# Four graph layers on one core: layer 2 of the last two batch pairs as passes of their own, quarter sums made earlier, a planner with other costs

## The chip, the cores and the metric

The kernel runs on one core of one Trainium2 chip. The metric is the device time of one execution in microseconds. Besides the timed runs there is one execution taken by the hardware profiler; views of it are quoted with times from the start of its span. Engines: PE (TensorE), DVE (VectorE), ACT (ScalarE), POOL and SP (which here only issue DMAs).

## The reference

Eight batches of 2048 nodes with 64 channels pass through four residual layers that share one 2048 x 2048 matrix `adj`. All is float32. Cut to what matters:

```python
# layer 0: Chebyshev graph convolution, node-adaptive weights (16 terms per node)
x_g = [x, A @ x, 2 A (A x) - x];  out = sum_d emb[n,d] * (x_g @ weight[d]) + bias
x = layernorm(x + out)
# layer 1: graph attention
e = leaky_relu(s1[:, None] + s2[None, :]); e[adj <= 0.5] = -9e15
x = layernorm(x + elu(softmax(e) @ x))
# layer 2: mean over neighbours
x = layernorm(x + ((adj + I) @ (x @ W.T + b)) / deg)
# layer 3: three steps, node 0 overwritten first
v = x;  v[:, 0] = iv
for _ in range(3):
    v = relu(concat([v, adj @ v]) @ W1.T + b1) @ W2.T + b2
x = layernorm(x + v)
```

## The kernel before

**Tiles.** Batches are taken in four pairs (`NPAIR`), so that two batches of 64 channels fill 128 columns. A slot such as `SX[p]` holds pair p's 2048 nodes as 16 tiles of 128 x 128. A product with the matrix is a *sweep*: the transposed matrix is streamed from HBM in 32 tiles of 128 x 2 x 512 (512 KB each, `fetch`, issued by SP into `a_ring`), chunk by chunk of 512 output nodes (`NCH` = 4) and eight tiles a chunk. Each tile serves two matmuls of 512 columns, each of which the profile shows as two instructions. The result of a chunk stands in one PSUM buffer of `acc_ring` (two) until an evict step copies it out.

**Order of the sweeps** (`sweeps`): first product of layer 0 for pairs 0 and 1 together (`masks=True`: DVE also makes the attention mask and adj + I from each tile); then the second product of pair p = 0 to 3, with the first product of pair p + 1 beside it where there is one left; then, for pairs 0 and 1, one sweep of layer 2 and three of layer 3. The last two pairs (`JOINT`) go together: `joint_layer2` (L1205) takes four matrix tiles at a time, one from each quarter of the matrix, and runs both pairs over each of them; `joint_layer3` (L1277, L1292) does the three steps of layer 3 with seven products of quarters instead of eight. It needs four sums and differences of the quarters (s1 to s4). `sums` (L1165, L1167) makes them on DVE during the joint layer 2 pass and POOL stores them in DRAM. Where a tile holds adj + I instead of adj, `pure` (L1148) fetches it once more.

**Between the sweeps.** `second_pass` (L593) multiplies each node tile by 16 weight blocks; `add_terms` scales the 16 results by the node's embedding and adds them. With a free buffer of `e_ring` (four of 128 x 2048), ACT writes 16 scaled terms (L616) and DVE adds them in a tree (L630, L632); without one, DVE adds each straight to `SX` (L618). For pair 0, ACT makes eight terms and DVE the other eight. `y2_evict` holds a chunk in one of two `yt_ring` buffers until the second pass is through with it. `layer1` and `scores` (L724, the row maxima, with masks loaded into `mr_ring`), `weights` (L802, L810, L815, L818, and the product L828) and `finish` (L863 to L902) are the attention layer. `layer2_tail` (L974, L983), `start_chunk` (norm, transposes L1008, then `u_chunk` L1021), `h_evict` (L946) and `last_chunk` (L1041) follow the sweeps of layers 2 and 3.

**Order of the instructions.** Nothing is ordered by the compiler. All steps are generators that `yield` an engine and what they wait for; `Plan` keeps a model time for each engine and each event, always starts the step that can begin earliest, and among equals the one of the lowest rank, and so fixes the order on every engine's queue. `plan.run(engine, cost, *after)` books a cost. For PE it adds `SLACK` to the time at which a step counts as ready. `sweeps` has rank 1000, so sweeps fill what PE has left. On the chip each engine works through its queue in that order and waits at semaphores.

Of the kernel before, what the change touches and what calls it, by code (L numbers as in the profile page):

```python
# [9 lines left out]
F32 = mybir.dt.float32  # L10
# [7 lines left out]
P = 128  # L18
# [19 lines left out]
class Plan:  # L38
# [6 lines left out]
    SLACK = 2.5  # L45

    def __init__(self):
        self.free = dict.fromkeys(["PE", "DVE", "ACT", "DMA", "SP"], 0.0)
        self.at = {}
        self.threads = []  # L50
        self.count = itertools.count()
# [8 lines left out]
    def run(self, eng, cost, *after):  # L60
        t = max([self.free[eng], *(self.when(a) for a in after)]) + cost
        assert t < NEVER
        self.free[eng] = t
        return t + self.LAG

# [70 lines left out]
def resnorm_d4_kernel(  # L136
# [44 lines left out]
    mr_ring = Ring(wp, "mr", 2)  # L181
# [36 lines left out]
    A_BUFS = 7  # L218
# [7 lines left out]
    def fetch(n):  # L226
        c, q, plus = order_of_a[n]
        t, k = a_ring.take([P, 2, CW], "a")
        freed = a_ring.t
        if isinstance(c, str):  # L230
            src = sum_tiles[c][q]
        else:
            src = a_plus_i[q] if plus and c == q // 2 else tile_of_adj(c, q)
        nc.sync.dma_start(t, src)
        a_tiles[n] = (t, k)
        at["a", n] = plan.run("SP", 1.4, freed) + 3.5
# [23 lines left out]
    blocks = ("w2bd", "w31v", "w31e", "w32bd", "w32c")  # L260
    w2bd, w31v, w31e, w32bd, w32c = (const.tile([P, P], F32, name=n) for n in blocks)
# [107 lines left out]
    def weights_of_l23():  # L369
# [20 lines left out]
        pp_ring.give(k, done)  # L390
        yield "PE", [pp_ring, done]
# [19 lines left out]
    def rows_of_adj():  # L411


        for t in range(NT):
# [4 lines left out]
            done = plan.run("SP", 2.8, bc_ring.t, 115.0 + 9.0 * t) + 9.0  # L419
            plan.start(1, row_tile(t, an, k, done))  # L420

    def row_tile(t, an, k, done):
# [9 lines left out]
        done = plan.run("DVE", 1.13 + 0.16, done)  # L432
        bc_ring.give(k, done)
        nc.gpsimd.dma_start(by_row[t], mk)
        done = plan.run("DMA", 0.6, done) + 4.0
        mr_ring.give(km, done)
        at["by_row", t] = done + 2.0
        if all(("by_row", i) in at for i in range(NT)):
            at["rows"] = done

    def mask_of_tile(n, t, k):
# [7 lines left out]
        if c == q // 2:  # L449
# [6 lines left out]
            got = plan.run("DMA", 0.6, got) + 4.0  # L456
        a_ring.give(k, max(done, got))
        nc.gpsimd.dma_start(by_col[q][:, :, cols(c)], mk)
        done = plan.run("DMA", 0.8, done) + 4.0
        mk_ring.give(km, done)  # L460
        at["by_col", q, c] = done + 2.0

    def layer_norm(v, n, after, centered=False):
# [4 lines left out]
        if not centered:  # L468
# [7 lines left out]
            done = plan.run("DVE", dve(n, 2) + 0.1, after)  # L476
# [9 lines left out]
        done = plan.run("DVE", dve(n) + 0.1, done)  # L486
# [5 lines left out]
        done = plan.run("ACT", 0.3, done)  # L492
        yield "DVE", [done]

        nc.vector.tensor_tensor(vs, vs, r, ALU.mult)
        nc.vector.scalar_tensor_tensor(vs, vs, -0.5, r, ALU.mult, ALU.mult)
        nc.vector.scalar_tensor_tensor(r, vs, 1.5, r, ALU.add, ALU.mult)
        nc.vector.tensor_tensor(v3, v3, r.unsqueeze(2).to_broadcast([P, nb, C]), ALU.mult)
        return plan.run("DVE", dve(n) + 0.4, done)
# [7 lines left out]
    def y1_chunk(p, c, pa, ka, done):  # L507
# [6 lines left out]
        stored = plan.run("DMA", 0.6, done) + 3.0  # L514
        at["y1T", p, c] = stored + 2.0
# [22 lines left out]

    def stacks():

        for n in range(NPAIR * NCH):
            p, c = n // NCH, n % NCH
# [5 lines left out]
            got = plan.run("DMA", 0.6, xg_ring.t, ("y1T", p, c)) + 4.0  # L548
# [15 lines left out]
    def second_pass():  # L564

        for n in range(NPAIR * NCH):
# [4 lines left out]
            for j in range(TPC):  # L571
                t = c * TPC + j
                cs = slice(j * P, (j + 1) * P)
                for h in range(2):
# [5 lines left out]
                    if h == 0 or ring.ready() > plan.free["PE"]:  # L580
                        yield "PE", [("xg", n + 1), got, ring]
                    if h == 0:


                        terms = None
                        if e_ring.ready() < NEVER:
                            terms = e_ring.take([P, D0, P], "terms")
# [17 lines left out]
    def add_terms(p, c, t, h, yp, ring, k, terms, t_pe, left):  # L605

        shared = p == 0 and terms is not None
        eng = "ACT" if terms and not (shared and h) else "DVE"
        yield eng, [t_pe]
        v = SX[p][:, t, :]  # L610
        for d in range(8):
# [5 lines left out]
            else:  # L617
                nc.vector.scalar_tensor_tensor(  # L618
                    batches(v), term, weight, batches(v), ALU.mult, ALU.add
                )  # L620
        done = plan.run(eng, 8 * (0.25 if eng == "ACT" else 0.265), t_pe)
# [4 lines left out]
        if terms:  # L626
            yield "DVE", [done, ("terms", p, t)]
            for half in (4, 2) if shared else (8, 4, 2):
                a, b = (terms[0][:, i * half : (i + 1) * half, :] for i in range(2))
                nc.vector.tensor_tensor(a, a, b, ALU.add)  # L630
            for d in range(2):
                nc.vector.tensor_tensor(v, v, terms[0][:, d, :], ALU.add)  # L632
            done = plan.run("DVE", 1.4 if shared else 2.5, done, ("terms", p, t))
            e_ring.give(terms[1], done)
# [18 lines left out]
    def layer1(p):  # L653
# [7 lines left out]
        for c in range(NCH):  # L661
# [30 lines left out]
        plan.start(10 + p, scores(p, sv, xc, s_rows, done))  # L692

    def scores(p, sv, xc, s_rows, done):
        s2b = []
        for e in range(2):
            yield "DMA", [bc_ring, done, "rows"]
# [4 lines left out]
            ready = plan.run("DMA", 0.8, done, bc_ring.t) + 7.5  # L702
# [6 lines left out]
        def load(t):  # L709
# [4 lines left out]
            at["mask", p, t] = plan.run("DMA", 0.6, mr_ring.t, ("by_row", t)) + 5.0  # L714

        plan.start(1, load(0))
        for h in range(2):
            mx = tiny([P, 2, 8], "mx", 4)
            for t in range(8 * h, 8 * h + 8):
                if t + 1 < NT:  # L720
                    plan.start(1, load(t + 1))
# [20 lines left out]
    def greatest(p, h, mx, sv, xc, s_rows, done):  # L742
# [5 lines left out]
        done = plan.run("DVE", 0.16, done)  # L748
# [7 lines left out]
        for name, rows in (  # L756
# [7 lines left out]
            ready = plan.run("DMA", 0.8, done, bc_ring.t) + 8.0  # L764
# [7 lines left out]
    def to_rows(v, rows, done):  # L772
# [12 lines left out]
        done = plan.run("DMA", 0.5, done) + 2.5  # L785
# [5 lines left out]
    def weights(p, h, jt, s1b, mb, sv, po, ready):  # L791
# [6 lines left out]
        got = plan.run("DMA", 0.6, mk_ring.t) + 4.5  # L798
# [14 lines left out]
        done = plan.run("ACT", act(HALF, 2), done)  # L813
# [6 lines left out]
        mine = held.setdefault((p, h), [])  # L820
        mine.append((jt, e, ke, done))
        if jt % 2 == 0:
            return
        yield "PE", [mine[0][3], done, *([("weighed", p, h, jt - 2)] if jt > 1 else [])]
# [14 lines left out]
        mine.clear()  # L839
# [6 lines left out]
    def finish(p, h, po, kpo, xc):  # L846
# [11 lines left out]
        for f in range(2):  # L858
# [24 lines left out]
            done = plan.run("DVE", dve(CW) + 0.12, t_pe)  # L883
# [21 lines left out]
            done = plan.run("DVE", dve(CW, 2) + 0.2, done)  # L905
# [3 lines left out]
        if h == 0:  # L909
            yield "DMA", [("weighted", p, 1)]  # L910
            nc.gpsimd.dma_start(SX[p][:, 0:8, :], stage)
            done = plan.run("DMA", 1.5, *norms) + 3.0
# [22 lines left out]
    def z_evict(p, c, pa, give, done):  # L935
# [4 lines left out]
        give(done)  # L940
# [29 lines left out]
    def layer2_tail(p, c, z, kz, done):  # L970
# [19 lines left out]
        done = plan.run("DVE", dve(P, TPC) + dve(CW), done)  # L990
# [46 lines left out]
    def last_chunk(p, c, done):  # L1037
# [15 lines left out]
        done = plan.run("DVE", dve(CW, 2), done)  # L1053
# [74 lines left out]
    def order_of_joint():  # L1128
        for k in range(2):
            for r in range(RQ):  # L1130
                order_of_a.extend((c, q, True) for c, q in quarters(k, r))
# [10 lines left out]
    def pure(k, r):  # L1142

        yield "SP", [("group", k, r), *([xg_ring] if len(xg_ring.freed) > 1 else [NEVER])]
        got = []
        for c, q in (quarters(k, r)[i] for i in (0, 3)):
            t, kt = xg_ring.take([P, 2, CW], "pure")
            nc.sync.dma_start(t, tile_of_adj(c, q))  # L1148
            got.append((t, kt, plan.run("SP", 1.4, xg_ring.t) + 4.0))
        return got  # L1150

    def sums(k, r, taken):

        tiles4 = [(t, kt, got) for t, kt, got, _ in taken]
        own = {}
        if r // 2 == k:
            own = dict(zip((0, 3), (yield from pure(k, r))))
        a11, a12, a21, a22 = ((own.get(i) or tiles4[i])[0] for i in range(4))
        ready = [(own.get(i) or tiles4[i])[2] for i in range(4)]

        def out_of(m, a, b, op, *after):
            yield "DVE", [bc_ring, *after]
            t, kt = bc_ring.take([P, 2, HALF], m)
            t = t.rearrange("p a b -> p (a b)")[:, 0 : 2 * CW].rearrange("p (t n) -> p t n", n=CW)
            nc.vector.tensor_tensor(t, a, b, op)  # L1165
            done = plan.run("DVE", dve(2 * CW), *after)
            nc.gpsimd.dma_start(sum_tiles[m][k, r], t)  # L1167
            bc_ring.give(kt, plan.run("DMA", 0.6, done) + 5.0)
            return t, done

        s3, d3 = yield from out_of("s3", a11, a21, ALU.subtract, ready[0], ready[2])
        s1, d1 = yield from out_of("s1", a21, a22, ALU.add, ready[2], ready[3])
        s2, d2 = yield from out_of("s2", s1, a11, ALU.subtract, d1)
        s4, d4 = yield from out_of("s4", a12, s2, ALU.subtract, d2)
        for (_, kt, _, free), d in zip(taken, (d2, d4, d1, d1)):
            a_ring.give(kt, max(free, d))
        for _, kt, _ in own.values():
            xg_ring.give(kt, d2)
        refill()

    def joint_layer2():
        p, o = JOINT
        at["group", 0, 0] = 0.0
        for k in range(2):
            pas = {}
            for r in range(RQ):
                taken = []
                for i, (c, q) in enumerate(quarters(k, r)):
                    n = next(used)
                    if r == 0 and i in (0, 2):  # L1190
                        if i == 0:
                            yield "PE", [po_ring, ("x2", p), ("x2", o)]
                            t2, kp = po_ring.take([P, 2, CW], "po")
                            pas[c] = [(t2[:, e, :], kp) for e in range(2)]
                        else:
                            pas[c] = []
                            for e in range(2):
                                yield "PE", [acc_ring]
                                pas[c].append(acc_ring.take([P, CW], "acc"))
                    for e, pair in enumerate(JOINT):  # L1200
                        yield "PE", [("a", n)]
                        t, kt = a_tiles[n]
# [268 lines left out]
```

## Time and profile before

| | us |
|---|---|
| median of 3 runs | 2172.77 (2169.68 to 2172.82) |
| the profiled execution | 2177.32 |
| its span | 2175.5 |
| PE / DVE / ACT busy in it | 2090.3 / 1532.3 / 933.5 |
| granted TensorE clock in it, mean | 0.984 |

In the profile the sweeps lie so: the first products 6 to 130 us, second products (with the next pair's first) 130 to 944, layer 2 and 3 of pair 0 944 to 1325, of pair 1 to 1685, joint layer 2 1688 to 1814, joint layer 3 to 2163. Attention of the four pairs runs on DVE and ACT from 351 to about 1700. In a line of a group, "x" is the count, then come busy time, the mean of one in ns, and the idle time of the engine before. A matmul's shown length overlaps its successor's; their pace is read from start to start.

### The profile page before, as it was taken

The page shows a single profiled execution, that of the slowest core. Times are in us where ns is not written, and L with a number is a line of the kernel's source. Part 1 is how long each engine was busy: PE and PEld are TensorE (multiplying, and loading weights), DVE is VectorE, ACT ScalarE, POOL GpSimd, SP SyncE. Part 2 cuts the span into 40 slices and gives each one's busy share as a digit, 9 for nine tenths or more (in the row PEclk, how much of TensorE's full clock was granted, in tenths as well). Part 3 has the DMA queues.
Part 4 walks back from the last instruction along what each step waited for, and adds up shares of the span by engine and source line. Part 5 has one row for each costly group of instructions (what it writes and reads, how often), then busy time and mean ns, then how long its engine had stood idle before and what let it go on. Part 6 is the DMA issues. An engine that isn't in the chain of part 4 may idle for free. (4 is left out here: it accounts for less than half of the span.)

```text
span 2175.5 us, 19004 instructions
## 1 busy us (share of the span) xinstructions
PE 2090.3 (96%) x6325; PEld 923.0 (42%) x6325; DVE 1532.3 (70%) x2057; ACT 933.5 (43%) x1605; POOL 213.3 (10%) x374
## 2 busy tenths in 40 slices
PE   8998999999999999999998999989999998999997
PEld 3443444333433333344443444434444454444443
DVE  2226756999799999979998978989797555020214
ACT  0014433476576457767624746417566012000001
POOL 2211001100110110001001011011100110000000
PEclk9999999999999999999999999989999999999999
DMA  9798845633542475446688788778687687878785
GB/s 313 270 328 305 287 133 184 216 107 96 162 150 88 150 234 153 146 126 198 223 289 299 247 286 294 233 249 303 220 293 226 238 301 243 281 251 282 252 291 169
DMA packets 208739, 495.85 MB, mean 228 GB/s; under 512 B 20274, under 2 KB 28594, under 8 KB 204530
## 3 DMA queue, kind: packets, MB, share of 16 engines
q1 hardware_dynamic: 165058, 347.62, 48.3%
q0 software_dynamic: 39360, 144.92, 19.4%
q10 hardware_dynamic: 4224, 2.10, 0.4%
q8 instruction: 50, 0.82, 0.1%
q14 instruction: 47, 0.39, 0.1%
HBM read 446.14 MB, written 46.33 MB: 226 GB/s over the span
## 5 line engine op out<-in xcount | busy, mean ns | idle before, releaser
L1086 PE MATMUL acc<-a,SX 128*128 128x512 f32 x1024 | 470.1, 603 | 9.0 <-DMA SX<-in_x 6.4
L1086 PE MATMUL acc<-a,SA 128*128 128x512 f32 x768 | 352.9, 602 | 8.0 <-ACT SA L348 4.7
L810 ACT ACTIVATE e<-e,sv 128x1024 f32<-128x1024 f32 x256 | 280.4, 1153 | 123.6 <-DVE e L802 117.3
L724 DVE CUSTOM_DVE_ANT_0 junk<-s2b,mr 128x2048 bf16<-128x2048 f32 x128 | 292.7, 2287 | 32.6 <-DMA mr<-by_row 31.3
L818 ACT ACTIVATE e<-e 128x2048 f32<-128x2048 f32 x128 | 245.3, 1925 | 120.5 <-DVE e L815 120.2
L802 DVE TENSOR_TENSOR e<-s1b,mk 128x2048 f32<-128x2048 f32 x128 | 289.6, 2284 | 9.8 <-DMA mk<-by_col 9.8
L815 DVE TENSOR_TENSOR e<-e,mb 128x2048 f32<-128x2048 f32 x128 | 290.2, 2284 | 7.6 <-ACT e L810 7.5
L1086 PEld LDWEIGHTS acc<-a,SX 128*128 128x128 f32 x1024 | 191.7, 193 | 242.7 <-issue 229.1
L593 PE MATMUL yp<-SH,xgT 128*128 128x512 f32 x512 | 250.7, 615 | 1.8 <-DVE SX L618 1.0
L616 ACT ACTIVATE terms<-yp,emb_sb 128x128 f32<-128x128 f32 x768 | 207.9, 396 | 70.9 <-PE yp L593 70.6
L828 PE MATMUL po<-e,SX 128*64 128x512 f32 x1024 | 234.0, 599 | 3.0 <-ACT e L818 3.0
L1086 PEld LDWEIGHTS acc<-a,SA 128*128 128x128 f32 x768 | 142.6, 192 | 182.0 <-issue 168.3
L1292 PE MATMUL acc<-a,t 128*128 128x512 f32 x384 | 169.1, 592 | 0.0
L593 PEld LDWEIGHTS yp<-SH,xgT 128*128 128x128 f32 x512 | 92.4, 193 | 147.6 <-issue 139.0
L593 PE MATMUL yp<-SH,y2T 64*128 64x512 f32 x512 | 134.9, 634 | 17.3 <-ACT terms L616 9.8
L630 DVE TENSOR_TENSOR terms<-terms 128x512 f32<-128x512 f32 (+1 forms) x152 | 111.2, 731 | 35.6 <-ACT terms L616 32.2
L828 PEld LDWEIGHTS po<-e,SX 128*64 128x64 f32 x1024 | 68.0, 137 | 155.6 <-issue 137.8
L797 POOL DMA_DIRECT2D mk<-by_col x128 | 69.3, 542 | 589.4 <-DVE e L802 475.9
L618 DVE SCALAR_TENSOR_TENSOR SX<-yp,emb_sb,SX 128x128 f32<-128x128 f32 x256 | 89.7, 350 | 48.9 <-PE yp L593 40.4
L1086 PE MATMUL acc<-a,SB 128*128 128x512 f32 x256 | 120.1, 601 | 0.0
L1292 PEld LDWEIGHTS acc<-a,t 128*128 128x128 f32 x384 | 72.0, 190 | 86.1 <-issue 86.1
L480 ACT ACTIVATE ln_sq<-SX 128x512 f32<-128x512 f32 x48 | 30.4, 633 | 146.4 <-DVE SX L473 81.1
(226 smaller groups left out, 1704.2 us busy)
## 6 DMA issues: line engine op xcount, KB each, us to landing
a<-in_adj_t SPq DMA_DIRECT2D x496, 512.0 KB, 5.3
a<-s SPq DMA_DIRECT2D x96, 512.0 KB, 4.5
mr<-by_row POOLq DMA_DIRECT2D x64, 512.0 KB, 5.9
mk<-by_col POOLq DMA_DIRECT2D x128, 256.0 KB, 5.6
an<-in_adj SPq DMA_DIRECT2D x16, 1024.0 KB, 9.3
s<-s POOLq DMA_DIRECT2D x32, 512.0 KB, 6.9
a<-a_plus_i SPq DMA_DIRECT2D x24, 512.0 KB, 5.7
by_col<-mk POOLq DMA_DIRECT2D x32, 256.0 KB, 6.1
```

The lines of the kernel that those rows point to most:

```text
L593: nc.tensor.matmul(yp[:, e, :], lhsT=y2T[rows, cs] if k2 else xg[:, e, cs], rhs=(wk2 if k2 else w01)[rows, hs], start=(k2 == h), stop=(k2 ...
L616: nc.scalar.activation(batches(terms[0][:, dd, :]), term, AF.Copy, scale=weight)
L618: nc.vector.scalar_tensor_tensor(batches(v), term, weight, batches(v), ALU.mult, ALU.add)
L630: nc.vector.tensor_tensor(a, a, b, ALU.add)
L724: nc.vector.tensor_tensor_reduce(out=junk, in0=s2b[e][0], in1=masks[t][0], scale=1.0, scalar=LOWEST, op0=ALU.add, op1=ALU.max, accum_out=m ...
L802: nc.vector.tensor_tensor(e, s1b[0], mk.unsqueeze(1).to_broadcast([P, 2, HALF]), ALU.add)
L810: nc.scalar.activation(e[:, i, :], e[:, i, :], AF.Prelu, bias=sv[:, 2 + i, jt : jt + 1], alpha=ALPHA)
L815: nc.vector.tensor_tensor(e, e, mb[0], ALU.add)
L818: nc.scalar.activation(e, e, AF.Exp)
L828: nc.tensor.matmul(po[i * C : (i + 1) * C, f, :], lhsT=SX[p][:, t, i * C : (i + 1) * C], rhs=e[:, i, f * CW : (f + 1) * CW], start=(t == 0 ...
L1086: nc.tensor.matmul(pa, lhsT=source[:, m, :], rhs=t[:, i, :], start=(m == 0 and not seed), stop=(m == NT - 1),)
L1292: nc.tensor.matmul(pa, lhsT=B[:, 2 * r + b, :], rhs=at_[:, b, :], start=(r == 0 and b == 0 and not go_on), stop=(r == RQ - 1 and b == 1), ...
```

## The change

Layer 2 of pairs 2 and 3 becomes two ordinary sweeps. The sums of quarters are made in place, in the tiles themselves, during the second product of pair 3 (`SUMS`), which for that takes the tiles by quarters and finishes chunks 0 and 2, then 1 and 3. `a_ring` goes from seven buffers to six, `mr_ring` from two to three. The second pass always has a terms buffer and waits for it; the tree of adds becomes one reduction over the 16 (or 8) terms. In the norm, a DVE multiplication becomes a squaring on ACT. `Plan` gets a model of shared DMA bandwidth, other costs, a smaller `SLACK` and other ranks. Of the cost changes only some are shown.

```diff
     LAG = 0.3
-    SLACK = 2.5
+    RATE = 340.0
+    SLACK = 1.0
...
+    def dma(self, queue, kb, *after):
+        t = self.run(queue, 0.4 if queue == "SP" else 0.7, *after) - self.LAG
+        self.moved = max(t + 3.5, self.moved) + kb / self.RATE
+        return self.moved + 0.2
...
-    mr_ring = Ring(wp, "mr", 2)
+    mr_ring = Ring(wp, "mr", 3)
...
-    A_BUFS = 7
+    A_BUFS = 6
...
-        at["a", n] = plan.run("SP", 1.4, freed) + 3.5
+        at["a", n] = plan.dma("SP", 512, freed)
...
         nc.scalar.activation(r, r, AF.Exp, scale=-0.5)
-        done = plan.run("ACT", 0.3, done)
+        rr = tiny([P, nb], "ln_rr", 2)
+        nc.scalar.activation(rr, r, AF.Square)
+        done = plan.run("ACT", 0.55, done)
         yield "DVE", [done]
-        nc.vector.tensor_tensor(vs, vs, r, ALU.mult)
-        nc.vector.scalar_tensor_tensor(vs, vs, -0.5, r, ALU.mult, ALU.mult)
+        nc.vector.scalar_tensor_tensor(vs, vs, -0.5, rr, ALU.mult, ALU.mult)
...
                     if h == 0 or ring.ready() > plan.free["PE"]:
-                        yield "PE", [("xg", n + 1), got, ring]
+                        yield "PE", [("xg", n + 1), got, ring, *([e_ring] if h == 0 else [])]
                     if h == 0:
-                        terms = None
-                        if e_ring.ready() < NEVER:
-                            terms = e_ring.take([P, D0, P], "terms")
+                        terms = e_ring.take([P, D0, P], "terms")
...
-        shared = p == 0 and terms is not None
-        eng = "ACT" if terms and not (shared and h) else "DVE"
+        shared = p == 0
+        eng = "DVE" if shared and h else "ACT"
...
-                nc.vector.scalar_tensor_tensor(
-                    batches(v), term, weight, batches(v), ALU.mult, ALU.add
-                )
+                to = batches(terms[0][:, d, :])
+                nc.vector.scalar_tensor_tensor(to, term, weight, to, ALU.mult, ALU.add)
...
-            for half in (4, 2) if shared else (8, 4, 2):
-                a, b = (terms[0][:, i * half : (i + 1) * half, :] for i in range(2))
-                nc.vector.tensor_tensor(a, a, b, ALU.add)
-            for d in range(2):
-                nc.vector.tensor_tensor(v, v, terms[0][:, d, :], ALU.add)
+        n = 8 if shared else D0
+        added = tiny([P, P], "added", 1)
+        nc.vector.tensor_reduce(
+            added, terms[0][:, 0:n, :].rearrange("p d n -> p n d"), AX.X, ALU.add
+        )
+        nc.vector.tensor_tensor(v, v, added, ALU.add)
...
-        plan.start(10 + p, scores(p, sv, xc, s_rows, done))
+        plan.start(1.2 if p == 0 else 9.5 + p, scores(p, sv, xc, s_rows, done))
...
-            yield "DMA", [bc_ring, done, "rows"]
+            yield "DMA", [bc_ring, done]
...
         plan.start(1, load(0))
+        plan.start(1, load(1))
...
+    def sweep_with_sums(source, evict, need):
+        for k in range(2):
+            pas = {}
+            for r in range(RQ):
+                group = []
+                for i, (c, q) in enumerate(quarters(k, r)):
+                    n = next(used)
+                    if r == 0 and i in (0, 2):
+                        yield "PE", [acc_ring]
+                        pas[c] = acc_ring.take([P, CW], "acc")
+                    yield "PE", [("a", n), *need(q // 2)]
+                    t, kt = a_tiles.pop(n)
+                    for b in range(2):
+                        nc.tensor.matmul(
+                            pas[c][0],
+                            lhsT=source[:, 2 * q + b, :],
+                            rhs=t[:, b, :],
+                            start=(r == 0 and i in (0, 2) and b == 0),
+                            stop=(r == RQ - 1 and i in (1, 3) and b == 1),
+                        )
+                    done = plan.run("PE", mm(CW, 2), ("a", n), *need(q // 2))
+                    if r == RQ - 1 and i in (1, 3):
+                        plan.start(1, evict(c, *pas[c], done))
+                    group.append((t, kt, done))
+                    if i == 3:
+                        plan.start(0, sums(k, r, group))
+                    refill()
+
+    def sums(k, r, group):
+        (a11, _, d11), (a12, _, d12), (a21, _, d21), (a22, _, d22) = group
+        for i, m, out, a, b, op, after in (
+            (3, "s1", a22, a21, a22, ALU.add, (d21, d22)),
+            (2, "s3", a21, a11, a21, ALU.subtract, (d11, d21)),
+            (0, "s2", a11, a22, a11, ALU.subtract, (d11,)),
+            (1, "s4", a12, a12, a11, ALU.subtract, (d12,)),
+        ):
+            yield "DVE", after
+            nc.vector.tensor_tensor(out, a, b, op)
+            done = plan.run("DVE", dve(2 * CW) + 0.03, *after)
+            nc.gpsimd.dma_start(sum_tiles[m][k, r], out)
+            a_ring.give(group[i][1], plan.dma("DMA", 512, done))
+        refill()
...
             products = [second_product(p)]
+            if p == SUMS:
+                yield from sweep_with_sums(*second_product(p)[0:3])
+                continue
...
+        yield from sweep(layer2_product(NPAIR - 2))
         yield "PE", [("x2", NPAIR - 1)]
         h_o, _ = e_ring.take([P, 2, HALF], "h_o")
-        yield from joint_layer2()
+        yield from sweep(layer2_product(NPAIR - 1))
         yield from joint_layer3()
```

## The prediction

> **What bounds the kernel now.** I read the page first (busy shares and the forty slices), then busy time by stage, then the waits of PE, then the timeline of PE around the stage that is rebuilt, and last the groups by shape, for prices.
>
> The page: PE is busy nearly everywhere, DVE only from about slice 7 to 31.
>
> ```profile
> PE 2090.3 (96%) x6325; PEld 923.0 (42%) x6325; DVE 1532.3 (70%) x2057; ACT 933.5 (43%) x1605; POOL 213.3 (10%) x374
> ...
> PE   8998999999999999999998999989999998999997
> DVE  2226756999799999979998978989797555020214
> ```
>
> Busy time by stage (window, its length, then PE, PEld, DVE, ACT, POOL busy, granted clock, DMA share, GB/s):
>
> ```profile
> 150.00:350.00 200.00, 193.49 (x563) 82.74 (x561) 120.70 (x311) 85.41 (x227) 14.54 (x25) 0.98 0.71 249
> 350.00:1050.00 700.00, 679.95 (x2084) 274.82 (x2084) 650.49 (x816) 443.80 (x912) 71.24 (x129) 0.99 0.49 156
> 1050.00:1684.00 634.00, 607.34 (x1963) 269.06 (x1960) 560.72 (x550) 337.74 (x339) 67.82 (x122) 0.98 0.77 263
> 1684.00:1850.00 166.00, 154.22 (x483) 80.23 (x482) 90.12 (x172) 26.32 (x60) 17.87 (x33) 0.96 0.75 260
> 1850.00:2176.00 326.00, 314.12 (x874) 150.72 (x872) 75.60 (x138) 27.83 (x52) 6.04 (x8) 0.99 0.77 254
> ```
>
> PE idles 6.5, 20.1, 26.7, 11.8 and 11.9 us in these stages, 85 us in all with the start. The change neither adds nor removes a product: joint layer 2 is 128 matmuls, two passes are 2 x 64. So PE's work stays, and only its idle time and what follows it can move. The waits of PE (total, times, longest):
>
> ```profile
> PE yp L593 <- ACT terms L616: 10.6, 6, 5.7
> PE ps_vT L1008 <- DVE SX L498: 8.3, 2, 6.8
> ...
> PE ps_u L1021 <- ACT SH L946: 5.2, 1, 5.2
> ...
> PE po L1205 <- DVE SX L498: 3.4, 1, 3.4
> ```
>
> The second and last of these lie at the two ends of the joint pass. PE's timeline there (start, length, group, idle before):
>
> ```profile
> 1688.12 5.31 PE L1205 MATMUL po<-a,SX 128*128 128x512 f32 x12
> 1696.81 2.65 PE L1205 MATMUL po<-a,SX 128*128 128x512 f32 x4 [3.37 <-DVE SX L498]
> 1699.25 8.11 PE L1205 MATMUL acc<-a,SX 128*128 128x512 f32 x16
> 1707.19 7.03 PE L1205 MATMUL po<-a,SX 128*128 128x512 f32 x16
> ...
> 1818.34 1.05 PE L974 MATMUL ps_emb<-w2bd,z 128*128 128x128 f32 x8
> 1826.20 2.32 PE L1008 MATMUL ps_vT<-ident,SX 128*128 128x128 f32 x8 [6.81 <-DVE SX L498]
> 1829.96 2.08 PE L1021 MATMUL ps_u<-w31e,SH 128*128 128x128 f32 x8 [1.44 <-ACT SH L348]
> ```
>
> An undisturbed run of 16 takes 6.87 us start to start (1707.19 to the next group), 0.429 per instruction; the 16 after the first wait take 7.94. A wait like this one is followed by a slow stretch and costs more than itself.
>
> **1. The ends of the joint pass.** At the front, 1688.12 to 1707.19 is 19.07 us for 32 instructions worth 13.73: 5.3 us lost to pair 3's last norm (x2 of the last pair). Afterwards PE has pair 2's layer 2 to run instead, 128 instructions or 55 us, so x2 may come up to some 50 us later unseen. At the back, from 1819.2 (the four ps_emb groups done) to 1834.4 (steady again) are 15.2 us for 12 transposes at 0.11 and 16 ps_u at 0.112, 3.1 us: 12.1 lost, because both pairs' last chunks must pass copy, norm, transpose and u before the first product can go on. Afterwards the first two products of layer 3 read pair 2's u alone, made a pass earlier; they hold 64 instructions, 27.5 us, over the 15 us chain of pair 3's last chunk. I take both away: **-17.4 us**. If the cover fails, the same 12 come back.
>
> **2. The sums on DVE.** 32 subtractions and additions of 128x1024 move from the joint pass, where DVE idles, to the sweep of pair 3 (771 to 944 in the timeline), where it is 95% busy: 32 x 1.22 = 39 us. They go at rank 0, ahead of terms and weights. DVE is relieved in the second pass at the same time. Prices:
>
> ```profile
> L618 DVE SCALAR_TENSOR_TENSOR SX<-yp,emb_sb,SX 128x128 f32<-128x128 f32 x256 | 89.7, 350 | 48.9 <-PE yp L593 40.4
> L630 DVE TENSOR_TENSOR terms<-terms 128x1024 f32<-128x1024 f32 x40 | 48.8, 1219 | 32.3 <-ACT terms L616 32.2
> L632 DVE TENSOR_TENSOR SX<-SX,terms 128x128 f32<-128x128 f32 x112 | 32.7, 292 | 3.9
> L1165 DVE TENSOR_TENSOR s<-a,s 128x1024 f32<-128x1024 f32 x8 | 9.8, 1224 | 1.3 <-DMA s<-s 1.2
> ```
>
> A tile's tree of adds is 1.219 + 0.689 + 0.425 (the other two shapes of L630) + 2 x 0.292 = 2.92 us. One reduction of 2048 elements has no row; the nearest are the 2048-element addition (2.28) and the reduction of 512 (0.68), so 2.28, and 2.57 with its addition. 40 tiles x 0.35 = 14 us less. Eight tiles that had no buffer go from 16 x 0.35 = 5.6 to 2.57: 24 less, against 128 more ACT instructions at 0.27 = 35 us on an engine busy 43%. Pair 0's sixteen: 3 less. Each of 64 norms loses a DVE instruction of 0.16 and gains one of 0.21 on ACT. Up to 1050 us DVE is therefore even: 39 - 14 - 24 - 3 - 4 = -6.
>
> The reduction reads its 16 terms 512 bytes apart. The trace has one DVE instruction with such a step, the copy of each batch's last column (32 elements, 256 bytes apart):
>
> ```profile
> L686 DVE COPY xc<-SX x4: 184/188/192, 330.9 to 1314.7; 128x32 f32<-128x32 f32 x4
> ```
>
> From additions of 512 (0.690) and 2048 (2.284) an element costs 1.04 ns and an instruction 158; 32 elements would be 191, and double price per element 224. It took 188, so I charge no step; the dear end is sixteen separate 128x128 additions, 16 x 0.292 = 4.67 us a tile, 2.1 more. The Trainium skill speaks against this ("Advanced Engine Details and Errata", SBUF Cachelines): an access that lands on another 16-byte line each time pays a penalty. It gives no figure; were the penalty a doubling, an estimate from that rule, the sum on DVE would be +100 instead of -6. The row, though short, shows no penalty.
>
> **3. Who waits for PE's sake.** A second-pass tile must now find an e buffer before it starts, where before it took one that was not yet free or went to DVE directly. That answers yp <- ACT terms (10.6), ps_xg <- ACT terms (2.2), ps_sv <- ACT terms (0.7), yp and ps_xg <- DVE SX (1.9 and 2.4): 17.8 us with the slow stretches on top, 25 at most; but the 5.7 at 196 us is in pair 0's pass, which stays. Bounds 0 and -25, I take **-9**.
>
> **4. Buffers.** In the quarter sweep four tiles are held together until four sums (4.9 us) and a store (s<-s lands after 6.9) are over, 11.8 us in which two of six buffers serve, 3.4 us of matmuls. Eight groups x 8.4 = 67 us if PE had nothing else. In the stretch 771 to 944 this sweep was 55 us of PE's 173; the rest is second pass and weights. By that share 21 us would show; most can be fetched while PE does the rest: bounds 0 and 67, I take **+5**. Six buffers instead of seven in the first sweep, where DMA is at 0.94 to 0.98 for 75 us and the matrix waits are 5.8 us in the whole run: 0 to +6, **+1**. The matrix is fetched 32 times more, 16.8 MB, and the 8 pure fetches on SP go; a dense pass needs 0.524 MB per 1.72 us = 305 GB/s, and 293 was moved without a wait in 1875 to 1900 us.
>
> **5. Scores of pair 0 ahead of the terms (rank 10 to 1.2), a third mr buffer.** Their 32 x 2.29 = 73 us can now run as one block from 351 us. Meanwhile pair 1's reductions wait, its four e buffers fill, and PE has 4 tiles x 5.4 + some 34 us of sweep before two yT buffers are used up: 56 of 73. Bounds 0 and +20, **+4**.
>
> **6. The order as a whole.** PE's margin goes from 2.5 to 1.0 us, most costs are raised by 0.1 to 0.35 and DMAs share a modelled 340 GB/s. Of the 47 us idle between 350 and 1684, part comes from work that the plan put too early. The smaller margin pulls the other way. No row prices it: bounds -35 and +25, I take **-10**.
>
> Sum: -17.4 - 9 + 5 + 1 + 4 - 10 = -26.4. The profiled execution took 2177.3 (span 2175.5), so 2150.9; it is 4.5 above the median of the runs, so I say **2147 us**.
>
> **Rivals.** (a) *Buffers decide, slower.* Place: the quarter sweep. Price 67 us in full. It decides once over 26 of them (40%) show; at 70%, 2147 + 42 = 2189. For: DVE is 95% busy there, and a late sum holds four of six buffers. Against: two thirds of PE's work there needs none. 20%. (b) *The score block gives the gain back*: 20 us instead of 4, and the plan's 10 not gained: 2147 + 16 + 10 = 2173, no change. 6%. (c) *The reduction costs as much as separate additions*: 48 x 2.1 + 16 x (8 x 0.292 - 1.51) = 114 us more of DVE before 1050; it idles 50 there from 350 on, so the second pass ends some 65 later; if PE's later fillers hide a third, 2147 + 43 = 2190. 6%. (d) The forecast, with the ends of the joint pass gone: 68%, 2115 to 2165 alone.
>
> Against a resolution of 0.2% (4.3 us) this gives faster 0.68, same 0.06, slower 0.26. The range 2110 to 2196 leaves out the far end of (a) and (c) and a plan that gains all of its 35.
>
> **What would show it.** Right: no wait of ps_vT on DVE before the first layer-3 product, no wait of pair 2's layer 2 on x2; L616 x896, one reduction per tile near 2.28 us; PE idle under 15 us in the last 500 us. Wrong: PE waits on a<- behind sums, a reduction of 4 us or more, an idle PE between 380 and 430, or idle between 350 and 1684 over 60 us.

## The result: slower by 0.5%, and where the profile after puts it

The changed kernel takes 2180.86 us (median of 5 runs, 2180.01 to 2183.67), before 2172.77 (2168.69 to 2173.97); the ratio is 1.0046, 95% interval 1.0034 to 1.0058. The forecast was 2147 and faster. Its profiled execution took 2183.67 us, span 2181.9.

Busy time by stage in the changed kernel, columns as in the prediction:

```profile
350.00:1050.00 700.00, 648.06 (x1937) 259.90 (x1935) 659.92 (x549) 434.61 (x966) 80.25 (x146) 0.97 0.49 166
1050.00:1684.00 634.00, 617.55 (x2010) 275.03 (x2009) 575.73 (x557) 354.43 (x401) 71.15 (x129) 0.98 0.78 270
1684.00:1850.00 166.00, 166.00 (x545) 81.18 (x544) 73.14 (x140) 53.75 (x92) 2.81 (x5) 1.00 0.76 250
```

Two stages got better as forecast: PE's idle time falls from 26.7 to 16.5 us between 1050 and 1684, and from 11.8 to nothing up to 1850. But between 350 and 1050 us it rises from 20.1 to 51.9, and the granted clock falls from 0.99 to 0.97. All that was gained and some 10 us more is lost there.

The timeline of PE at what used to be the ends of the joint pass (start, length, group; a wait would stand in brackets):

```profile
1728.71 10.46 PE L1095 MATMUL acc<-a,SX 128*128 128x512 f32 x24
1739.01 1.05 PE L872 MATMUL pf<-back,poT 128*128 128x130 f32 x8
...
1841.31 8.75 PE L1246 MATMUL acc<-a,SA 128*128 128x512 f32 x20
1849.90 0.60 PE L1017 MATMUL ps_vT<-ident,SX 128*128 128x128 f32 x4
```

Pair 2's layer 2 runs while pair 3's attention finishes (pf), and pair 3's last transposes (1849.90) come in the midst of layer 3's first products. Neither waits. PE's waits are now others:

```profile
PE acc L1162 <- DMA a<-in_adj_t: 13.0, 6, 9.8
PE po L838 <- ACT e L827: 10.9, 6, 4.5
...
PE ps_y L529 <- ACT y1T L358: 7.5, 4, 6.7
PE yp L602 <- ACT terms L625: 6.5, 6, 2.2
```

L1162 is the quarter sweep. Before, all waits for tiles of the transposed matrix together were these:

```profile
PE acc L1086 <- DMA a<-in_adj_t: 5.8, 7, 1.7
```

The groups of DVE by shape show what changed there and in the whole second pass:

```profile
L637 DVE TENSOR_REDUCE added<-terms 128x128 f32<-128x2048 f32 x48 | 177.1, 3690 | 42.1 <-ACT terms L625 41.7
L1188 DVE TENSOR_TENSOR a<-a 128x1024 f32<-128x1024 f32 x32 | 39.1, 1223 | 0.8
L637 DVE TENSOR_REDUCE added<-terms 128x128 f32<-128x1024 f32 x16 | 30.7, 1921 | 0.2
```

The sums cost the 39 us they were put at. The reduction of 16 terms takes 3.69 us, not 2.28, and that of eight 1.92. Both are 1.72 ns per element over 158 ns. Against the forecast that is 48 x 1.41 + 16 x 0.70 = 79 us more of DVE before the second pass ends. The longest wait for a matrix tile (9.83 us, ended at 830.98) has such reductions in front of it, on DVE's own timeline:

```profile
807.41 3.69 DVE L637 TENSOR_REDUCE added<-terms 128x128 f32<-128x2048 f32 x1
...
812.35 4.49 DVE L824 TENSOR_TENSOR e<-e,mb 128x2048 f32<-128x2048 f32 x2
...
817.48 3.75 DVE L637 TENSOR_REDUCE added<-terms 128x128 f32<-128x2048 f32 x1
821.27 0.29 DVE L640 TENSOR_TENSOR SX<-SX,added 128x128 f32<-128x128 f32 x1
821.48 1.22 DVE L1188 TENSOR_TENSOR a<-a 128x1024 f32<-128x1024 f32 x1
```

The sums of that group start at 821.48, after PE had begun to wait at 821.15; their tiles come free one by one from then on.

### The profile page after: what moved, and what is told of

The parts are those of the page before. It is cut to its first block, busy times and chain, and to the rows that moved or that the text cites. A ratio compares the mean times of both kernels' runs of the same rounds, so it can differ in the third digit from the quotient of the medians.

```text
span 2181.9 us, 18920 instructions
## 1 busy us (share of the span) xinstructions
PE 2090.0 (96%) x6325; PEld 920.2 (42%) x6325; DVE 1553.2 (71%) x1728; ACT 981.3 (45%) x1798; POOL 213.4 (10%) x374
## 5 line engine op out<-in xcount | busy, mean ns | idle before, releaser
L1095 PE MATMUL acc<-a,SX 128*128 128x512 f32 x1280 | 586.1, 602 | 12.0 <-DMA SX<-in_x 6.5
L1095 PEld LDWEIGHTS acc<-a,SX 128*128 128x128 f32 x1280 | 238.4, 193 | 298.9 <-issue 278.3
L625 ACT ACTIVATE terms<-yp,emb_sb 128x128 f32<-128x128 f32 x896 | 242.7, 396 | 106.1 <-PE yp L602 101.3
L838 PE MATMUL po<-e,SX 128*64 128x512 f32 x1024 | 240.0, 610 | 10.9 <-ACT e L827 10.9
L637 DVE TENSOR_REDUCE added<-terms 128x128 f32<-128x2048 f32 (+1 forms) x64 | 207.9, 3248 | 42.3 <-ACT terms L625 41.7
L602 PE MATMUL yp<-SH,y2T 64*128 64x512 f32 x512 | 129.6, 620 | 3.8 <-ACT terms L625 2.3
L602 PEld LDWEIGHTS yp<-SH,y2T 64*128 64x128 f32 x512 | 43.7, 187 | 86.6 <-issue 77.4
L1162 PE MATMUL acc<-a,SB 128*128 128x512 f32 x128 | 61.4, 616 | 13.0 <-DMA a<-in_adj_t 13.0
```

Source lines behind the costliest of these rows:

```text
L602: nc.tensor.matmul(yp[:, e, :], lhsT=y2T[rows, cs] if k2 else xg[:, e, cs], rhs=(wk2 if k2 else w01)[rows, hs], start=(k2 == h), stop=(k2 ...
L625: nc.scalar.activation(batches(terms[0][:, dd, :]), term, AF.Copy, scale=weight)
L637: nc.vector.tensor_reduce(added, terms[0][:, 0:n, :].rearrange("p d n -> p n d"), AX.X, ALU.add)
L838: nc.tensor.matmul(po[i * C : (i + 1) * C, f, :], lhsT=SX[p][:, t, i * C : (i + 1) * C], rhs=e[:, i, f * CW : (f + 1) * CW], start=(t == 0 ...
L1095: nc.tensor.matmul(pa, lhsT=source[:, m, :], rhs=t[:, i, :], start=(m == 0 and not seed), stop=(m == NT - 1),)
```

## The experiments

Three theories: A, the reduction's price; B, the sums in the quarter sweep and the four buffers they hold; C, the new order itself. Each ratio is against the kernel before, which was timed again with each group of experiments (medians 2170.7 to 2172.3 us); differences between two experiments are those of their medians.

**e1: the tree back.** Same order on PE and ACT.

```diff
-        nc.vector.tensor_reduce(
-            added, terms[0][:, 0:n, :].rearrange("p d n -> p n d"), AX.X, ALU.add
-        )
-        nc.vector.tensor_tensor(v, v, added, ALU.add)
+        for half in (4, 2) if shared else (8, 4, 2):
+            a, b = (terms[0][:, i * half : (i + 1) * half, :] for i in range(2))
+            nc.vector.tensor_tensor(a, a, b, ALU.add)
+        for d in range(2):
+            nc.vector.tensor_tensor(v, v, terms[0][:, d, :], ALU.add)
```

> The changed kernel with the one reduction per tile replaced by the old tree of adds; the planned cost is left, so the order on PE and ACT is the same and on DVE only these instructions differ. Theory A (the strided reduction is the cause: 3.69 us measured for 16 terms and 1.92 for 8, where the tree is 2.92 and 1.70 with its last adds): DVE is relieved of 48 x 1.06 + 16 x 0.5 = 59 us before 1060 us, PE's idle time between 350 and 1050 us falls from 52 us to 20 to 35, and the time to 2150 to 2165. Theory B (sums and buffers of the quarter sweep): the waits for matrix tiles in that sweep stay at 13 us with the 9.8 us one, and the time stays within 2175 to 2183. Theory C (the order: scores of pair 0 first, small margin): the time stays too, and idle time between 400 and 750 us stays near 22 us.

Measured: 2141.13 us, ratio 0.986 (0.9842 to 0.9877). The stretch from 350 to 1050, and the groups of the tree:

```profile
350.00:1050.00 700.00, 677.92 (x2071) 275.41 (x2070) 647.73 (x721) 466.24 (x1027) 85.51 (x156) 0.99 0.55 179
```

```profile
L638 DVE TENSOR_TENSOR terms<-terms 128x1024 f32<-128x1024 f32 x48 | 58.5, 1219 | 42.3 <-ACT terms L625 42.0
L638 DVE TENSOR_TENSOR terms<-terms 128x512 f32<-128x512 f32 x64 | 44.2, 690 | 1.9
...
L640 DVE TENSOR_TENSOR SX<-SX,terms 128x128 f32<-128x128 f32 x128 | 37.4, 292 | 4.4
...
L638 DVE TENSOR_TENSOR terms<-terms 128x256 f32<-128x256 f32 x64 | 27.2, 425 | 2.2
```

PE's idle time there is 22.1 us. The tree is 167 us of DVE, where the reductions (208) and their additions (19) are 227. One instruction's replacement takes 40 us off and turns a slower kernel into a faster one: theory A, and by more than I put it at. The quarter sweep's waits for tiles are still 10.1 us, so something of B is left.

**e2: the joint pass back, reduction kept.** `joint_layer2`, `pure` and the old `sums` in the changed kernel, with the costs of the new planner.

> The changed kernel with the joint layer 2 pass of before, its sums at their old place and their old buffers; planner, ranks, reduction and the six buffers stay changed. If the passes and the early sums gain what was forecast for them (17 us at the ends, less 5 for the buffers), this is 5 to 15 us slower than the changed kernel: 2186 to 2196. Theory B (early sums cost more than the ends give back): it is faster, 2160 to 2175, and PE's idle time between 350 and 1050 us falls by over 15 us. Theories A and C: idle time in that stretch stays at 45 to 55 us.

Measured: 2183.08 us, ratio 1.0048 (1.0032 to 1.0064), the same as the changed kernel within the intervals. Idle time between 350 and 1050 is 31.0 us, 21 less, but 11.2 us are back between 1684 and 1850 and 24.0 stand between 1050 and 1684. So the passes and early sums neither gained nor lost here: what the ends gave, the second pass took. Neither branch of my expectation held.

**e3: the passes and early sums alone, on the kernel before.**

> The kernel before with only the two layer 2 passes and the in-place sums in pair 3's quarter sweep; its planner costs, margin, ranks, tree of adds and seven buffers stay. My forecast for this part alone: 2172 - 17 + 5 = 2160. Theory B: 2172 or more, with waits for matrix tiles behind the sums of 10 us and over. Theories A and C: 2155 to 2165, idle time between 1684 and 1850 us gone (from 11.8 to under 2).

Measured: 2156.4 us, ratio 0.9929 (0.9912 to 0.9946), 14 us where I had 12. Idle time between 1684 and 1850 us is gone as expected, and waits for matrix tiles total 6.8 us outside the quarter sweep, none in it. Between 350 and 1050 PE idles 30.6 us against 20.1; whether the sums or the new order cost that, this run does not tell.

**e4: ranks of the scores back.**

```diff
-        plan.start(1.2 if p == 0 else 9.5 + p, scores(p, sv, xc, s_rows, done))
+        plan.start(10 + p, scores(p, sv, xc, s_rows, done))
```

> The changed kernel with the ranks of the scores as before (10 + p instead of 1.2 and 9.5 + p). Theory C: the block of pair 0's scores from 331 to 418 us is broken up again and the time falls by 5 us or more, to 2175 or less. Theories A and B: within 5 us of 2180, with the idle time between 350 and 1050 us at 45 to 55.

Measured: 2184.38 us, ratio 1.0054 (1.0037 to 1.0071). No better; idle time in the stretch is 59.1 us. So the block of pair 0's scores does not explain the loss.

**e5: the step of the reduction.** The buffer is laid out as n = (h, l) with the term in between, `"p (h d l) -> p h l d"` for the reduction, with l = 128, 64, 4 and 1 floats for pairs 0 to 3.

> The changed kernel with the same order and the same reductions, but another layout of the 16 scaled terms: the reduction steps through them at 512 bytes for pair 0 (as in the changed kernel), 256 bytes for pair 1, 16 for pair 2 and 4 (side by side) for pair 3; ACT writes with the step instead. Theory step: 2048 elements take 3.7 us at 256 and 512 bytes, and fall to the 2.28 us of an addition of 2048 for the terms side by side; at 16 bytes either, which tells where the step begins to cost. Rival, the form of a reduction with 128 results: 3.7 us in all three pairs. If the step is the cause and the writes cost ACT nothing, the time falls by half to two thirds of what the tree gained, to 2150 to 2165; if ACT's instructions grow instead (0.39 us now), it falls less.

The groups of the reductions: L665 is pairs 1 and 2, L663 pair 3, L659 pair 0:

```profile
L665 DVE TENSOR_REDUCE added<-terms 128x128 f32<-128x2048 f32 x32 | 121.0, 3781 | 35.8 <-ACT terms L639 33.2 <-ACT terms L641 2.3
L663 DVE TENSOR_REDUCE added<-terms 128x128 f32<-128x2048 f32 x16 | 36.5, 2280 | 7.1 <-ACT terms L639 7.1
L659 DVE TENSOR_REDUCE added<-terms 128x128 f32<-128x1024 f32 x16 | 30.8, 1923 | 0.2
```

Side by side 2048 elements take 2.28 us, exactly an addition's price. Within L665, the sixteen of pair 1 (256 bytes) have a median of 3.67 us and those of pair 2 (16 bytes) 3.90. So the step is the cause, not the form, and it costs in full from 16 bytes on, perhaps earlier (8 was not tried). ACT's writes with a step show longer instructions (pair 3: median 491 ns instead of 394) but start 250 ns apart as before. The time is 2166.44 us, ratio 0.9986 (0.9969 to 1.0002): 14 us less than the changed kernel, from some 20 us of DVE (16 x 1.41 = 23 less in pair 3, 3 more in pair 2).

**e6: the plan told the real price.**

```diff
-        done = plan.run("DVE", dve(n * P) + dve(P) + 0.1, done)
+        done = plan.run("DVE", (2.1 if shared else 3.9) + dve(P) + 0.1, done)
```

> The changed kernel with the reduction as it is, but its measured price in the plan (3.9 and 2.1 us with its overhead instead of 2.2 and 1.14), so the order is made anew. If the loss is from an order built on a wrong price, the time falls to 2145 to 2160; if it is DVE's time itself, it stays at 2170 to 2185, and idle time of PE between 350 and 1050 us at 40 to 55.

Measured: 2173.16 us, ratio 1.0009 (0.9995 to 1.0023). The time lies in the branch of DVE's own time (2170 to 2185), though PE's idle time between 350 and 1050, 31.2 us, is below its 40 to 55. Of the 40 us a fifth comes back when the order knows the price, and a new order moves time by that much anyway (e8).

**e7: tree and joint pass, under the new planner.**

> The changed planner with the tree of adds and the joint layer 2 pass of before. With e1, e2 and the changed kernel it completes two by two. If the passes are worth with the tree what they were worth alone on the kernel before (14 us), this is 2155; if the reduction and the early sums only hurt each other, the tree gains here less than the 40 us it gained with the passes: 2150 to 2165; if the two are independent, it gains 40 as well: 2143.

Measured: 2138.63 us, ratio 0.9846 (0.9822 to 0.9871). The tree gains 44 us here and 40 with the passes: independent, and the passes are worth nothing under the new planner. It also shows what the rest of the change is worth: with reduction and passes both undone, costs, DMA model, waiting for a terms buffer (with the eight tiles that now find one), the squaring on ACT, ranks and rings make 33 us.

**e8: the tree with its own price in the plan** (3.0 and 1.75 us).

> The changed kernel with the tree of adds and the tree's own price in the plan (3.0 and 1.75 us): the version that should beat both. Against e1, whose plan takes 2.5 and 1.4 us for it: 2130 to 2145, 5 us or so better if wrong prices of half a microsecond matter, equal if they don't.

Measured: 2153.74 us, ratio 0.9919 (0.99 to 0.9939). The same instructions as e1 with the truer price, and 13 us slower. PE waits 23.8 us for weights (po <- ACT e) where e1 waits 8.2. A better price does not make a better order by itself; differences of some 13 us between two orders mean little.

**e9: the terms side by side for all pairs.** Same order as the changed kernel on all engines.

```diff
+        by_n = terms[0].rearrange("p d n -> p (d n)").rearrange("p (n d) -> p n d", d=D0)
...
-                nc.scalar.activation(batches(terms[0][:, dd, :]), term, AF.Copy, scale=weight)
+                nc.scalar.activation(by_n[:, :, dd].rearrange("p (b c) -> p b c", c=C), term, AF.Copy, scale=weight)
...
-                to = batches(terms[0][:, d, :])
+                to = by_n[:, :, d].rearrange("p (b c) -> p b c", c=C)
...
-            added, terms[0][:, 0:n, :].rearrange("p d n -> p n d"), AX.X, ALU.add
+            added, by_n[:, :, 0:n], AX.X, ALU.add
```

> The changed kernel in the same order, with the terms laid side by side for all four pairs (ACT and, for pair 0, DVE write with a step of 64 bytes, the reduction reads without one). The one change is the step. If the step is the whole loss: a reduction of 16 takes 2.28 us and of 8 about 1.2, a tile 2.57 against the tree's 2.92, and the time is that of e1 or up to 10 us better: 2130 to 2143. If the writes with a step cost DVE or ACT, the pair 0 instructions grow over 0.35 us and the time stays above 2145.

Measured: 2129.03 us, ratio 0.9798 (0.9777 to 0.9819): 2.0% faster than before, 52 us faster than the changed kernel, and the fastest that leaves nothing out. Its groups and its stretch of the second pass:

```profile
L626 ACT ACTIVATE terms<-yp,emb_sb 128x128 f32<-128x128 f32 x896 | 254.3, 496 | 120.0 <-PE yp L602 117.5 <-issue 2.3
L638 DVE TENSOR_REDUCE added<-terms 128x128 f32<-128x2048 f32 x48 | 109.5, 2281 | 44.5 <-ACT terms L626 42.9 <-ACT ln_r L499 1.3
L638 DVE TENSOR_REDUCE added<-terms 128x128 f32<-128x1024 f32 x16 | 19.4, 1214 | 0.2
```

```profile
350.00:1050.00 700.00, 686.03 (x2109) 279.98 (x2108) 643.25 (x608) 477.62 (x1040) 85.65 (x156) 0.99 0.54 181
1684.00:1850.00 166.00, 166.00 (x519) 84.11 (x518) 42.30 (x103) 26.67 (x60) 0.00 (x0) 1.00 0.80 266
```

PE idles 14.0 us between 350 and 1050, less than before the change. Pair 0's DVE writes did grow, from 342 to 438 ns each, so that part of my expectation's second branch held, but without its consequence.

**e10: side by side, joint pass.**

> The same layout with the joint layer 2 pass of before. After e1 and e7 (2141 and 2139) the passes seem to be worth nothing under the new planner: then this is within 6 us of e9. If the passes are worth the 14 us that they gained alone on the kernel before, this is 2145 to 2157.

Measured: 2130.86 us, ratio 0.9805 (0.9783 to 0.9827), 2 us from e9: the passes are worth nothing in a third pairing.

**e11: e1 without the 32 additions on DVE.**

```diff
-            nc.vector.tensor_tensor(out, a, b, op)
             done = plan.run("DVE", dve(2 * CW) + 0.03, *after)
```

> e1 (tree of adds, passes) in the same order, without the 32 additions on DVE: each tile is stored as it is, so layer 3 of the last two pairs computes with wrong quarters at the same cost. If DVE's 39 us for the sums are what takes back the gain of the passes, 10 to 20 us come free: 2121 to 2131, and the waits for tiles in the quarter sweep (10.1 us in e1) go. If it is the holding of four buffers through the store, the waits stay and the time is within 5 us of 2141.

Measured: 2118.47 us, ratio 0.9748 (0.9727 to 0.9769), 23 us under e1. The wait in the quarter sweep, first in e1, then here:

```profile
PE acc L1162 <- DMA a<-in_adj_t: 10.1, 5, 5.8
```

```profile
PE acc L1162 <- DMA a<-in_adj_t: 2.6, 1, 2.6
```

The four buffers are held through the store as before; what is gone is DVE's 39 us and the tiles' wait for their turn on it. So DVE, rather than the number of buffers, takes back what the ends give. Against e7, whose joint pass makes the sums where DVE idles, the passes without sums are 20 us faster, near the 17.4 forecast for the ends (the two orders differ, so some of it can be chance).

**e12: e1 with seven matrix buffers and two mask buffers.**

```diff
-    A_BUFS = 6
+    A_BUFS = 7
-    mr_ring = Ring(wp, "mr", 3)
+    mr_ring = Ring(wp, "mr", 2)
```

> e1 with seven matrix buffers and two mask buffers instead of six and three; the order is made anew. If the holding of buffers in the quarter sweep is what takes back the passes' gain, the waits there fall under 4 us and the time to 2125 to 2137. If not, 2135 to 2150, the spread that a new order alone gave between e1 and e8 (2141 and 2154).

Measured: 2147.15 us, ratio 0.9884 (0.9862 to 0.9906), in the branch of "not the buffers": the waits in that sweep are still 7.1 us.

## Why the prediction was wrong, step by step

**Step 2, the price of the reduction, is the step that failed.** I took 2.28 us from the nearest rows and let a copy of 32 elements with a step (188 ns) overrule the Trainium skill's "Advanced Engine Details and Errata", SBUF Cachelines, where an access that lands on another 16-byte line each time is penalised. The runs agree with the page: 1.04 ns per element side by side, 1.72 to 1.83 from 16 bytes on. The page has no figure; here the penalty is 1.7 times. The copy was misread: I set it beside the rate of an addition, but copies from SBUF to SBUF are faster than additions in the same trace (an addition of 128x128 takes 292 ns):

```profile
L999 DVE COPY v<-SX 128x128 f32<-128x128 f32 x3 | 0.7, 227 | 0.2
L315 DVE COPY back<-ident 128x128 f32<-128x128 f32 x1 | 0.2, 220 | 0.0
L316 DVE COPY back<-ident 128x2 f32<-128x2 f32 x1 | 0.2, 161 | 0.0
```

From 2 to 128 elements these rows give 0.47 to 0.52 ns an element, so 32 elements side by side would take some 176 ns and at double price per element some 190 (estimates from these rows). The 188 measured lies at the second: against its own kind the copy with a step did cost more. Whether by the same mechanism as the reduction the runs do not show, and 12 ns of one short row are little to build on. The estimate of +100 for a doubled price also left out pair 0's sixteen tiles; with them it is +113. I should have weighed the range, not the row: its dear end, 4.67 us a tile, was nearer to the 3.98 measured than the 2.57 I took.

**Rival (c) is what happened**, at 6%: 79 us of DVE instead of 114, and 2181 instead of 2190. Its mechanism held: the second pass ends at 1061.6 us instead of 1015.2, and PE's fillers hide a part; with the terms side by side (e9) it ends at 1013.0. The last products of that pass on PE, in the kernel before, in the changed one and in e9:

```profile
1013.24 1.98 PE L593 MATMUL yp<-SH,xgT 128*128 128x512 f32 x4
```

```profile
1059.61 1.98 PE L602 MATMUL yp<-SH,xgT 128*128 128x512 f32 x4
```

```profile
1011.01 1.98 PE L602 MATMUL yp<-SH,xgT 128*128 128x512 f32 x4
```

How large a part, four runs give: 59 us of DVE taken away gave 40 us (e1), 20 gave 14 (e5), 39 gave 23 (e11), and 79 less some 11 for pair 0's longer writes gave 52 (e9). So a microsecond of DVE before the end of the second pass is worth some 0.6 to 0.8 us here, in a kernel whose PE is 96% busy. Step 2's balance of -6 us would have been +73, at 0.6 some 45 us of time. That the rival's 2190 comes so near is partly luck: it put a loss of 43 us on 2147, and the runs show 52 on e9's 2129, so two misses offset each other.

**Step 1** was right in place and mechanism. Both waits are gone (11.8 us of idle time to none), with pair 2's pass in front and the first two products behind.

**Step 4** was right that the early sums cost something and wrong in what. I priced the buffers (5 of a possible 67). It is DVE's 39 us, worth 23 us of time in e11, and those offset the ends: e2, e7 and e10 put the passes at 2 us either way under the new planner. On the old one, e3, they are worth 14, which is no more than a new order alone moved (e8). I had counted the 39 us on DVE as even because the reduction, the eight tiles without a buffer and the norms were to pay for them.

**Step 3**, the terms buffer: yp <- ACT terms went from 10.6 to 6.5 us only, and ps_sv <- ACT terms from 0.7 to 4.2. With DVE relieved they are 1.2 and 0.9 (e1): right, but hidden by step 2. **Step 5**, scores first, was put at 4 us; e4 shows no loss from it, within what a new order moves. **Step 6**, the order as a whole, was put at -10. Steps 3, 5, 6 and the six buffers together I had at -14; e7 measures them, with the eight tiles that now find a buffer and the saving in the norms, at -33. The forecast without the failed step would have been too careful, since e9, which pays the price that I assumed, takes 2129 where I said 2147. Of the signs of being wrong two came: PE idle between 350 and 1684 for 68 us, over the 60 named, and waits for tiles behind the sums. PE's idle time in the last 500 us, 10 us, was as forecast.

What the runs leave open is why a truer price (e8) made a worse order than a wrong one (e1).

## What to carry to other kernels

Before a tree of contiguous adds becomes one reduction, ask how far apart the reduction reads; let the engine that has room (here ACT, whose writes still started 250 ns apart) write the operands side by side. A PE at 96% does not mean that other engines are free: read the stage, and ask what PE could do instead if that engine were late. An experiment that replaces one instruction and keeps the order tells more than one that makes the order anew, which alone moved this kernel by 13 us.

## What the hardware showed that I had not expected

Reading 4-byte elements on DVE at steps of 16, 256 and 512 bytes costs 1.72 to 1.83 ns each where neighbours cost 1.04, 16 bytes being the dearest and the others alike. Writing with a step of 64 bytes lengthened ACT's 128x128 instruction from 394 to about 490 ns and left its rate alone (a start every 250 ns); DVE's own 128x128 scalar_tensor_tensor, which takes one operand from PSUM and reads and writes the terms with that step, went from 342 to 438 ns, and from a start every 259 ns to one every 341.
